# Up results of three groups written as whole rows, and two times moved in the column plan

## The chip, the cores and the metric

The kernel runs on one core of a Trainium2 chip. The metric is the device time of one execution in microseconds (us), before 4126.9 (median of 3 runs, 4126.24 to 4131.73). The engines of the core are TensorE (PE in the profile, its weight loads PEld), VectorE (DVE), ScalarE (ACT), GpSimd (POOL) and SyncE (SP), which here only issues transfers. Each takes its own instructions in the order in which the program emits them, and waits for others by semaphores.

## The reference

Two layers, each `x = x + conv(gn(x))` with x of shape (32, 48, 64, 128): batch, channels, height, width. `gn` normalizes each image over 16 groups of 3 channels. `conv` is four scans, each with a one-dimensional convolution of 5 taps over the 48 channels:

```python
def f(carry, inp):
    nxt = inp + _conv1d(carry, w, b)
    return (nxt, nxt)
```

It runs down the 64 rows (the convolution lies along the width), then up through the down results with the same weights, then right through the 128 columns (the convolution lies along the height), then left. A step needs the step ahead of it, so each scan is a chain.

## The kernel before

The batch of 32 is cut into four groups of 8 images (g = 0 to 3). A layer has six phases in `PHASES`: four of kind "rows", one for each group (63 down steps, then 63 up steps), and two of kind "cols", for groups 0 and 1 (pair 0) and groups 2 and 3 (pair 1), each with 127 right and 127 left steps. The names of the tiles of a step say layer, group or pair and way: `step_01d` is layer 0, group 1, down; `step_11r` is layer 1, pair 1, right. In layer 1 the groups 1 to 3 run an up scan and the next down scan in joint steps (`JOINED`). A step is 9 matmuls (L899), whose sums VectorE joins with the bias and the input by `scalar_tensor_tensor` (L913) into the row or column in the `arena`, a tile of SBUF with three slots; the next step reads that.

Between phases the data lies in DRAM. `xin` holds the permuted input of a group and `in_x` is the kernel's input before it is permuted; `upa` (layer 0) and `upb` (layer 1) hold the up results, one tensor per group; `mid` holds layer 0's result; `spill` takes a quarter of a pair that has no room; `held` holds results of layer 1 that are sent to `out` later. Numbers behind such names in a listing tell buffers apart: `upa2_90` is group 2 of layer 0, `spill1_103` is the spill of its pair 1.

In a row phase `move_rows` writes up results out, eight rows at a time. The three output blocks of 128 partitions are cut into ten pieces of 16 to 48 channels (`PIECES`), one transfer for each piece. A row of 128 floats (16 columns of 8 images, for one of the eight residues of the column) is cut into four quarters `q` of RUN = 32 floats, and `by_row` puts each at its own place in DRAM, in runs of 128 bytes, so that a quarter of the width lies together.

In a column phase the pair is worked in quarters j of 32 columns, each of six units of 128 x 2048 floats: `UNITS` is (block o, half), half 0 the first group of the pair, half 1 the second. `load_unit` reads one unit of quarter j by `by_col`; a partition's 2048 floats lie together there, 8 KB. The three slots hold three quarters; the first is written to `spill` (`spill_unit`) once its columns have been passed, and the fourth quarter is loaded in its place. In layer 0, on the way left, the residual is loaded for each unit (`load_residual`, from `xin`), added on GpSimd (`add_residual`, L834), and the unit is written to `mid` (`keep_result`); then `pair_scaling` works out the normalization of layer 1. In layer 1 the result is permuted and stored; residuals are loaded by ScalarE's queue there.

What sets the order is an agenda: `at(t, fn, ...)` asks for a piece of work ahead of step t, counted over all phases, and ahead of each step the pieces that are due are emitted, sorted by t and then by the order of asking. The numbers set only the order on each engine's queue. An instruction starts when those ahead of it on its engine have been issued and its semaphores allow it; nothing waits for a step as such. SyncE's queue carries nearly all transfers: row loads, up writes, input loads, unit loads, spills, residuals, results.

`plan_rows` sets row loads, scaling (`scale_rows`, L777, on ScalarE) and the up writes; for groups 0 to 2 of layer 0 four of the eight up writes come during the up scan, at steps 12, 20, 28 and 36 of it, and four in the next group's down scan, at 30, 42, 54 and 66 behind its start. `plan_input` prepares the input of the next groups in the same phases: `take_in` loads 2048 KB from `in_x`, GpSimd permutes it (L699), SyncE puts it out to `xin`, and ScalarE takes statistics of it (`take_others`, L562 and L570). `plan_cols` sets, with t0 the first right step, `left` the first left step and `end` the step behind the last: loads of the four quarters, spills at t0 + 33 + 2i for unit i, and the adds, in the order of the quarters 3, 2, 1, 0, the units of the first three at left + 34 + 32n + 4.5i. `after` holds for a pair that follows a pair: pair 1, in both layers.

Of the kernel before, what the change touches and what calls it, by code (L numbers as in the profile page):

```python
# [42 lines left out]
E8 = 8  # L43
FULL = 128
NG = E8 * C // FULL
NQ = 4
# [31 lines left out]
def weight_runs():  # L78
# [24 lines left out]
PHASES = (  # L103
    ("rows", 0, 0),
    ("rows", 0, 1),
    ("rows", 0, 2),
    ("rows", 0, 3),
    ("cols", 0, 0),
    ("cols", 0, 1),
    ("rows", 1, 0),  # L110
    ("rows", 1, 1),
# [3 lines left out]
    ("cols", 1, 1),  # L115
)
JOINED = (8, 9)


@with_exitstack  # L120
def kernel(
# [11 lines left out]
    NH = H // E8  # L133
# [3 lines left out]
    RUN = KQ * GB  # L137
# [89 lines left out]
    def by_row(t, e, h0, h1):  # L227


        t = t.rearrange("c (i q a e n) -> e a c i q n", i=E8, q=NQ, a=NH, e=E8)[e, h0 // E8]  # L230
        t = t[:, h0 % E8 : h0 % E8 + h1 - h0]
        return t.rearrange("c i q n -> c (i q) n")

    def x_by_row(t, e, h0, h1):

        t = t.rearrange("(i q) c (a e n) -> e a c i q n", i=E8, a=NH, e=E8)[e, h0 // E8]
        return t[:, h0 % E8 : h0 % E8 + h1 - h0].rearrange("c i q n -> c (i q) n")
# [44 lines left out]
    def by_col(t, e, j):  # L282


        return t.rearrange("c (i q n) -> i q c n", i=E8, q=NQ)[e, j]

    def dma(dst, src, queue=None):
        (queue or nc.sync).dma_start(dst, src)
# [21 lines left out]
    def pieces(o):  # L310
        return [(e, c0, c1, p0) for e, c0, c1, g, p0 in PIECES if g == o]
# [404 lines left out]
    def place(k, h):  # L716


        first = k
        while first in JOINED:  # L720
            first -= 1
# [5 lines left out]
    def rows_at(k, h0, h1):  # L727

        places = sorted(place(k, h) for h in range(h0, h1, E8))
        at = places[0] * E8 + h0 % E8  # L730
        assert h0 // HALF == (h1 - 1) // HALF and places[-1] - places[0] == len(places) - 1
        return row_views(k)[h0 // HALF][:, :, at : at + h1 - h0]
# [4 lines left out]
    def move_rows(k, h0, h1, to_dram):  # L737

        _, layer, g = PHASES[k]
        t = (ups if to_dram else source)[layer][g]  # L740
        for h in range(h0, h1, E8):
            end = min(h1, h + E8)
            view = rows_at(k, h, end)
            for o in range(NG):
                for e, c0, c1, p0 in pieces(o):
                    here = view[p0 : p0 + c1 - c0, o]
                    here = here.rearrange("p h (q n) -> p (h q) n", q=NQ)
                    if to_dram:
                        dma(by_row(t, e, h, end)[c0:c1], here)
                    else:  # L750
                        dma(here, (x_by_row if g else natural_row)(t, e, h, end)[c0:c1])
# [41 lines left out]
    def quarter(k, j):  # L793
        return slot[slots(k)[j % 3]].rearrange("p (o s n) -> p s o n", s=2, o=NG)

    def load_unit(k, j, i):


        _, layer, pair = PHASES[k]
        o, half = UNITS[i]  # L800
        unit = quarter(k, j)[:, half, o]
        t = ups[layer][2 * pair + half]
        for e, c0, c1, p0 in pieces(o):
            here = unit[p0 : p0 + c1 - c0]
            dma(here, by_col(t, e, j)[c0:c1])

    def spill_unit(k, i, back):
        _, layer, pair = PHASES[k]
# [190 lines left out]
    def scans(k):  # L999
        if PHASES[k][0] == "rows":  # L1000
            if k not in JOINED:
                for h in range(1, H):
                    yield 1, lambda h=h: row_step(k, h, row(k, h - 1), row(k, h), "d")
            end = last.rearrange("p (o n) -> p o n", o=NG)
            for h in range(H - 2, -1, -1):
                if k + 1 in JOINED:
                    yield 2, lambda h=h: two_row_step(k, h, k + 1, H - 1 - h)
# [13 lines left out]
    def at(t, fn, *args):  # L1021
        agenda.append((t, len(agenda), fn, args))

    def spread(t, gen, every):


        def go(t):
            if next(gen, "end") != "end":
                at(t + every, go, t + every)
                agenda.sort(key=lambda a: a[:2])  # L1030

        at(t, go, t)
# [21 lines left out]
    def plan_rows(k, t0, prev):  # L1054
        layer = PHASES[k][1]
        down, up = (2 if k in JOINED else 1), (2 if k + 1 in JOINED else 1)
        t_up = t0 + down * (H - 1)
# [4 lines left out]
        else:  # L1062
            ahead, scaled = (-54, -43, 0, 11), (-22, -8, 16, 30)
            if not PHASES[k][1]:
                ahead, scaled = (-36, -26, 0, 11), (-18, -8, 16, 30)
        if k in JOINED:
            for i in range(H // E8):
# [32 lines left out]
    def plan_cols(k, t0, prev):  # L1100
        _, layer, pair = PHASES[k]
        n = 2 * NG
        after = prev == "cols"
        for i in range(n):
            early = 30 if after else 58 if k - 1 in JOINED else 54
            at(t0 - early + 2 * i, load_unit, k, 0, i)
            at(t0 + (3 if after else -24 + 2 * i), load_unit, k, 1, i)
            at(t0 + (38 if after else 8) + 2 * i, load_unit, k, 2, i)
            at(t0 + 33 + 2 * i, spill_unit, k, i, False)
            at(t0 + 50 + 2 * i, load_unit, k, 3, i)  # L1110
        final = k == len(PHASES) - 1
        left = t0 + W - 1
        end = left + W - 1
        for i in range(n):

            t = left + 64 + 2 * i if layer == 0 else left + 39.5 + 4.5 * i
            at(t, spill_unit, k, i, True)
        units = []
        for n_done, j in enumerate((3, 2, 1, 0)):
            first, every = left + 34 + 32 * n_done, 4.5  # L1120
            if j == 0 and PHASES[k + 1 if not final else k][0] == "rows":
                first, every = (end + 29, 6) if pair else (first, 7)
            units += [(first + every * i, j, i) for i in range(n)]
        stats = None
        if layer == 0:
            stats = ResultStatsV(f"r{2 * pair}"), ResultStatsA(f"r{2 * pair + 1}")
        tiles = [stage[:, i] for i in range(4)]
        if layer:
            tiles += spare_tiles[0 : 2 if final else 1]
        n = len(tiles)  # L1130
        direct = [u for u in units if not (final and u[1] == 0)]

        for u, (t, j, i) in enumerate(direct):
            nat = tiles[u % n]
            o, half = UNITS[i]
            if u < n:
                at(left + 16, load_residual, k, j, i, nat)
            if layer == 0:
                if u >= n:
                    at(max(direct[u - n][0] + 3, t - 21), load_residual, k, j, i, nat)  # L1140
                at(t, add_residual, k, j, i, nat)
                at(t + 4, keep_result, k, j, i)
                unit = quarter(k, j)[:, half, o]
                if half == 0:
                    for b in range(GB):
                        at(t + 5 + b, stats[0].take, j, o, unit, b)
                else:
                    at(t + 1, stats[1].take, j, o, unit)
            else:

                at(t, add_residual, k, j, i, nat)
                at(t + 2.5, permute_unit, k, j, i, nat, (nc.gpsimd, nc.scalar, nc.scalar))
                if final or j not in HELD:
                    at(t + 4.5, store_result, k, j, i, nat)
                else:
                    at(t + 4.5, hold_result, j, i, nat)
                if final and j == 1:
                    at(t + 4.7, load_residual, k, 0, i, last_tiles(k)[i])

                if u >= 2 and u - 2 + n < len(direct):  # L1160
                    at(t + 4.6, load_residual, k, *direct[u - 2 + n][1:], tiles[(u - 2) % n])
        if layer == 0:
            spread(units[-1][0] + 14, pair_scaling(pair, stats, 8), 1)
        if layer:

            at(left + 10, nc.scalar.copy, junk[:, BN - 1 :], quarter(k, 3)[:, 0, 0, RUN - 1 : RUN])
        if layer and not final:
            todo = [(j, half, e) for j in HELD for half in range(2) for e in range(E8)]
            for n, what in enumerate(todo):
                at(end + 63 + 1.9 * n, let_result, *what)  # L1170
        if final:
            at(end + 4, last_results, k)

    def last_tiles(k):

        s = slot[slots(k)[2]].rearrange("p (i n) -> p i n", i=2 * NG)
        return [s[:, i] for i in range(2 * NG)]
# [10 lines left out]
    starts, end = [], 0  # L1188
    for k, (kind, *_) in enumerate(PHASES):
        n = (H if kind == "rows" else W) - 1  # L1190
        starts.append(end - 2 * n if k in JOINED else end)
        end = starts[-1] + (2 if k in JOINED else 1) * n + (2 if k + 1 in JOINED else 1) * n
    for k, (kind, layer, _) in enumerate(PHASES):
        (plan_rows if kind == "rows" else plan_cols)(k, starts[k], PHASES[k - 1][0])
# [279 lines left out]
```

## Time and profile before

| | |
|---|---|
| median of 3 runs | 4126.9 us (4126.24 to 4131.73) |
| the profiled execution's own time | 4129.71 us |
| its span, first to last instruction | 4128.0 us |
| mean granted TensorE clock | 0.990 of full speed |
| moved by DMA | 681.57 MB, mean 165 GB/s |
| packets under 512 B | 2008848 of 2207818 |

The trace is one execution. Rows of a timeline give start, duration, engine, line, operation, result <- operands, the shape, a count where rows are joined, and in brackets the idle time ahead with what ended it. SPq is SyncE's queue: a row there is the time in which transfers were issued, not moved. Rows of waits give who waited <- for whom: total, count, longest, in us.

```profile
PE   6999999999999999999999999999999999999994
...
PEclk9999999999999999999999999999999999999997
DMA  9898998986990399814896965666698029999799
```

Each digit is a fortieth of the span, 103 us: TensorE works in all of them, and the DMA engines are nearly full in the first third (the row phases of layer 0) and by stretches later.

### The profile page before, as it was taken

The numbers are of one execution on the slowest core, as the hardware profiler recorded it, in microseconds if no ns is written. First come the engines' busy times: TensorE is split into PE (matmuls) and PEld (weight loads), VectorE is DVE, ScalarE is ACT, GpSimd is POOL, SyncE is SP. The second block draws the span as 40 slices with busy tenths as digits, with TensorE's granted clock in tenths as the row PEclk, the third lists the DMA queues.
The fourth block names the chain that finished last, engine by engine and source line by source line (L and its number), as shares of the span: only waits on it lengthen the run. The fifth ranks groups of instructions, "written<-read, shape, count | busy, mean of one in ns | idle before, by whom it ended". The sixth has DMA issues, their size and how long they took to land. (4 is left out here: it accounts for less than half of the span.)

```text
span 4128.0 us, 85199 instructions
## 1 busy us (share of the span) xinstructions
PE 4015.7 (97%) x34360; PEld 3930.1 (95%) x34360; DVE 2082.2 (50%) x6137; ACT 1307.0 (32%) x2628; POOL 789.3 (19%) x672
## 2 busy tenths in 40 slices
PE   6999999999999999999999999999999999999994
PEld 5999999999999999999999998888999999999994
DVE  6454454544444567545656443333444444444444
ACT  4556547450000256003674633434000002300122
POOL 5631303200000243002411000000000015610353
PEclk9999999999999999999999999999999999999997
DMA  9898998986990399814896965666698029999799
GB/s 300 217 203 171 222 157 211 208 132 116 165 226 1 89 261 285 210 20 151 217 171 146 141 107 95 100 108 100 100 171 205 1 70 252 294 246 157 148 233 195
DMA packets 2207818, 681.57 MB, mean 165 GB/s; under 512 B 2008848, under 2 KB 2157504, under 8 KB 2182080
## 3 DMA queue, kind: packets, MB, share of 16 engines
q1 hardware_dynamic: 2071488, 595.36, 69.7%
q10 hardware_dynamic: 135936, 80.77, 8.1%
q8 instruction: 270, 4.42, 0.5%
q14 instruction: 124, 1.02, 0.1%
HBM read 399.11 MB, written 295.93 MB: 168 GB/s over the span
## 5 line engine op out<-in xcount | busy, mean ns | idle before, releaser
L834 POOL TENSOR_TENSOR arena<-arena 128x2048 f32<-128x2048 f32 x80 | 362.5, 4548 | 1714.7 <-PE step_00l L899 499.9
L777 ACT ACTIVATE arena<-arena,offsetr,scaler 128x128 f32<-128x128 f32 (+1 forms) x576 | 345.1, 687 | 348.4 <-DMA arena<-mid 291.0
L638 ACT ACTIVATE early<-arena 128x256 f32<-128x256 f32 x192 | 129.7, 676 | 816.0 <-POOL arena L834 809.6
L777 ACT ACTIVATE arena<-arena,offset,scale 128x256 f32<-128x256 f32 (+2 forms) x360 | 248.8, 785 | 151.4 <-DMA arena<-xin 143.2
L699 POOL COPY arena<-arena 128x256 f32<-128x256 f32 x340 | 201.0, 658 | 443.1 <-DMA arena<-in_x 392.5
L899 PE MATMUL step_01r<-arena,early 128*128 128x128 f32 x2286 | 249.8, 272 | 0.0
L899 PE MATMUL step_11r<-arena,early 128*128 128x128 f32 x2286 | 249.3, 272 | 0.0
L899 PEld LDWEIGHTS step_11r<-arena,early 128*128 128x128 f32 x2286 | 248.7, 184 | 0.6 <-DVE arena L913 0.3
L899 PEld LDWEIGHTS step_01r<-arena,early 128*128 128x128 f32 x2286 | 248.9, 184 | 0.2
L899 PE MATMUL step_00r<-arena,early 128*128 128x128 f32 x2286 | 248.5, 272 | 0.0
L899 PE MATMUL step_10l<-arena,wleft 128*128 128x128 f32 x2286 | 248.5, 272 | 0.0
L899 PE MATMUL step_11l<-arena,wleft 128*128 128x128 f32 x2286 | 248.5, 272 | 0.0
L899 PE MATMUL step_10r<-arena,early 128*128 128x128 f32 x2286 | 248.5, 272 | 0.0
L899 PEld LDWEIGHTS step_00r<-arena,early 128*128 128x128 f32 x2286 | 248.5, 184 | 0.0
L899 PE MATMUL step_00l<-arena,wleft 128*128 128x128 f32 x2286 | 248.4, 272 | 0.0
L899 PE MATMUL step_01l<-arena,wleft 128*128 128x128 f32 x2286 | 248.4, 272 | 0.0
L899 PEld LDWEIGHTS step_10l<-arena,wleft 128*128 128x128 f32 x2286 | 248.4, 184 | 0.0
L899 PEld LDWEIGHTS step_11l<-arena,wleft 128*128 128x128 f32 x2286 | 248.4, 184 | 0.0
L899 PEld LDWEIGHTS step_10r<-arena,early 128*128 128x128 f32 x2286 | 248.4, 184 | 0.0
L899 PEld LDWEIGHTS step_00l<-arena,wleft 128*128 128x128 f32 x2286 | 248.4, 184 | 0.0
L899 PEld LDWEIGHTS step_01l<-arena,wleft 128*128 128x128 f32 x2286 | 248.4, 184 | 0.0
L856 ACT COPY arena<-arena 128x256 f32<-128x256 f32 x172 | 99.7, 657 | 367.1 <-POOL arena L834 241.0
(545 smaller groups left out, 6880.6 us busy)
## 6 DMA issues: line engine op xcount, KB each, us to landing
xin<-arena SPq DMA_DIRECT2D x94, 512.0 KB, 5.1
arena<-in_x SPq DMA_DIRECT2D x18, 2048.0 KB, 10.0
upa<-arena SPq DMA_DIRECT2D x192, 192.0 KB, 4.1
arena<-upa SPq DMA_DIRECT2D x96, 384.0 KB, 11.7
arena<-xin SPq DMA_DIRECT2D x96, 384.0 KB, 10.7
upb<-arena SPq DMA_DIRECT2D x192, 192.0 KB, 3.9
arena<-upb SPq DMA_DIRECT2D x96, 384.0 KB, 11.1
arena<-xin SPq DMA_DIRECT2D x174, 192.0 KB, 4.3
```

The source lines that it names most:

```text
L638: nc.scalar.activation(junk[:, 0:n], view[:, b], AF.Identity, accum_out=self.sum[:, i, j : j + 1])
L699: copy(dst[:, r, q], src[:, r0 + r, q])
L777: nc.scalar.activation(args[0], args[0], AF.Identity, bias=args[2], scale=args[1])
L834: eng.tensor_tensor(unit, unit, nat, ALU.add)
L856: copy(by_w(perm)[:, a], src[:, a])
L899: nc.tensor.matmul(part(turn(whole(ps[o]))[0:m], -s), weights[:, i, at : at + m], part(turn(src(i)), s), start=seen[o] == 1, stop=seen[o] ...
```

## The change

There are three edits.

1. `WHOLE` names groups 0, 1 and 2 of layer 0. Their up results are written with `whole_row`: a row's four quarters stay together, in runs of 512 bytes. Their units are then read with `part_of_rows`: one quarter of each of 64 rows for each partition, 64 runs of 128 bytes in place of one of 8 KB. Group 3 and layer 1 keep the old layout.
2. In `plan_cols` the third quarter of a pair that follows a pair is loaded at t0 + 46 + 2i in place of t0 + 38 + 2i. The condition holds in layer 0 and in layer 1.
3. The last quarter (j = 0) of pair 0 in layer 0 is added at end + 10 + 6.5i in place of end + 3 + 4.5i. Residual loads, results and `pair_scaling` are set from the same numbers and move with it. Pair 1 keeps end + 29 + 6i; in layer 1 the numbers come out as before.

The arithmetic and its operations are the same.

```diff
+WHOLE = ((0, 0), (0, 1), (0, 2))
...
+    def whole_row(t, e, h0, h1):
+        t = t.rearrange("c (i a e n) -> e a c i n", i=E8, a=NH, e=E8)[e, h0 // E8]
+        return t[:, h0 % E8 : h0 % E8 + h1 - h0]
...
+    def part_of_rows(t, e, j):
+        return t.rearrange("c (i m q n) -> i q c m n", i=E8, q=NQ, n=RUN)[e, j]
...
+                    if to_dram and (layer, g) in WHOLE:
+                        dma(whole_row(t, e, h, end)[c0:c1], here)
+                        continue
...
-            dma(here, by_col(t, e, j)[c0:c1])
+            if (layer, 2 * pair + half) in WHOLE:
+                dma(here.rearrange("p (m n) -> p m n", n=RUN), part_of_rows(t, e, j)[c0:c1])
+            else:
+                dma(here, by_col(t, e, j)[c0:c1])
...
-            at(t0 + (38 if after else 8) + 2 * i, load_unit, k, 2, i)
+            at(t0 + (46 if after else 8) + 2 * i, load_unit, k, 2, i)
...
-            if j == 0 and PHASES[k + 1 if not final else k][0] == "rows":
-                first, every = (end + 29, 6) if pair else (first, 7)
+            if j == 0 and layer == 0:
+                first, every = (end + 29, 6) if pair else (end + 10, 6.5)
```

In the listings below, x2 and the like is a count of equal rows. SyncE's queue in the up scan of group 0, layer 0, holds the first up write of eight rows (before, L288):

```order
L288 DMA upa0_88<-arena_72 48x32x32 x2
L288 DMA upa0_88<-arena_72 32x32x32
L288 DMA upa0_88<-arena_72 16x32x32
L288 DMA upa0_88<-arena_72 48x32x32 x2
L288 DMA upa0_88<-arena_72 16x32x32
L288 DMA upa0_88<-arena_72 48x32x32 x2
L288 DMA upa0_88<-arena_72 32x32x32
```

At the same place stands after the change (the line has moved to L298):

```order
L298 DMA upa0_88<-arena_72 48x8x128 x2
L298 DMA upa0_88<-arena_72 32x8x128
L298 DMA upa0_88<-arena_72 16x8x128
L298 DMA upa0_88<-arena_72 48x8x128 x2
L298 DMA upa0_88<-arena_72 16x8x128
L298 DMA upa0_88<-arena_72 48x8x128 x2
L298 DMA upa0_88<-arena_72 32x8x128
```

The same ten transfers with the same bytes, in runs of 128 floats for 32; nothing has moved.

SyncE's queue in the right scan of pair 1, layer 0 (`step_01r`), from the first spill of the first quarter on, before:

```order
L288 DMA spill1_103<-arena_72 128x2048 x3
L288 DMA arena_72<-upa2_90 48x2048 x2
L288 DMA arena_72<-upa2_90 32x2048
L288 DMA spill1_103<-arena_72 128x2048
L288 DMA arena_72<-upa3_91 48x2048 x2
L288 DMA arena_72<-upa3_91 32x2048
L288 DMA spill1_103<-arena_72 128x2048
L288 DMA arena_72<-upa2_90 16x2048
L288 DMA arena_72<-upa2_90 48x2048 x2
L288 DMA arena_72<-upa2_90 16x2048
L288 DMA spill1_103<-arena_72 128x2048
L288 DMA arena_72<-upa3_91 16x2048
```

And after, from the last two spills on (four spills and two results of pair 0 stand ahead of them):

```order
L298 DMA spill1_103<-arena_72 128x2048 x2
L298 DMA arena_72<-upa2_90 48x64x32 x2
L298 DMA arena_72<-upa2_90 32x64x32
L298 DMA mid1_85<-arena_72 96x8x256
L298 DMA mid1_85<-arena_72 32x8x256
L298 DMA arena_72<-upa3_91 48x2048 x2
L298 DMA arena_72<-upa3_91 32x2048
L298 DMA arena_72<-upa2_90 48x64x32 x2
L298 DMA arena_72<-upa2_90 32x64x32
L298 DMA arena_72<-upa2_90 16x64x32
L298 DMA arena_72<-upa2_90 48x64x32 x2
L298 DMA arena_72<-upa2_90 16x64x32
```

All six spills now stand ahead of the third quarter's loads, one result of pair 0 (`mid1`) stands behind its first unit, and the second pair of rows of group 2 (48 x2, 32) is already the fourth quarter's first unit: from there the units of the two quarters alternate, the third quarter's last one behind four of the fourth, where before all six of the third came first.

SyncE's queue in the right scan of pair 1, layer 1 (`step_11r`), from the first spill on, before:

```order
L288 DMA spill3_105<-arena_72 128x2048 x3
L288 DMA arena_72<-upb2_94 48x2048 x2
L288 DMA arena_72<-upb2_94 32x2048
L288 DMA spill3_105<-arena_72 128x2048
L288 DMA arena_72<-upb3_95 48x2048 x2
L288 DMA arena_72<-upb3_95 32x2048
L288 DMA spill3_105<-arena_72 128x2048
L288 DMA arena_72<-upb2_94 16x2048
L288 DMA arena_72<-upb2_94 48x2048 x2
L288 DMA arena_72<-upb2_94 16x2048
```

And after:

```order
L298 DMA spill3_105<-arena_72 128x2048 x6
L298 DMA arena_72<-upb2_94 48x2048 x2
L298 DMA arena_72<-upb2_94 32x2048
L298 DMA arena_72<-upb3_95 48x2048 x2
L298 DMA arena_72<-upb3_95 32x2048
L298 DMA arena_72<-upb2_94 48x2048 x2
L298 DMA arena_72<-upb2_94 32x2048
L298 DMA arena_72<-upb2_94 16x2048
L298 DMA arena_72<-upb2_94 48x2048 x2
L298 DMA arena_72<-upb2_94 16x2048
```

Here too the six spills come first and the two quarters' units alternate (the second 48 x2, 32 of upb2 is the fourth quarter's); the layout of upb is as before.

## Prediction

> **What bounds the kernel now.** The page's engine totals come first, then the waits of TensorE, then the starts of the phases in VectorE's timeline.
>
> ```profile
> PE 4015.7 (97%) x34360; PEld 3930.1 (95%) x34360; DVE 2082.2 (50%) x6137; ACT 1307.0 (32%) x2628; POOL 789.3 (19%) x672
> ...
> PE step_01d L899 <- DVE arena L913: 6.8, 1, 6.8
> PE step_02d L899 <- DVE arena L913: 5.4, 1, 5.4
> ...
> 326.00 1.14 DVE L913 SCALAR_TENSOR_TENSOR arena<-step_01d,bd,arena 128x128 f32<-128x128 f32 x3 [0.91 <-DMA arena<-xin]
> 459.03 0.61 DVE L913 SCALAR_TENSOR_TENSOR arena<-step_01u,bd,arena 128x128 f32<-128x128 f32 x2 [0.73 <-PE step_01u L899]
> 588.10 0.61 DVE L913 SCALAR_TENSOR_TENSOR arena<-step_02d,bd,arena 128x128 f32<-128x128 f32 x2 [0.79 <-PE step_02d L899]
> 719.53 0.61 DVE L913 SCALAR_TENSOR_TENSOR arena<-step_02u,bd,arena 128x128 f32<-128x128 f32 x2 [0.73 <-PE step_02u L899]
> 847.08 0.61 DVE L913 SCALAR_TENSOR_TENSOR arena<-step_03d,bd,arena 128x128 f32<-128x128 f32 x2 [0.79 <-PE step_03d L899]
> 971.45 0.61 DVE L913 SCALAR_TENSOR_TENSOR arena<-step_03u,bd,arena 128x128 f32<-128x128 f32 x2 [0.73 <-PE step_03u L899]
> 1095.94 0.65 DVE L913 SCALAR_TENSOR_TENSOR arena<-step_00r,bd,arena 128x128 f32<-128x128 f32 x2 [0.78 <-DMA upa<-arena]
> 1344.26 0.61 DVE L913 SCALAR_TENSOR_TENSOR arena<-step_00l,bd,arena 128x128 f32<-128x128 f32 x2 [0.71 <-PE step_00l L899]
> 1592.60 1.18 DVE L913 SCALAR_TENSOR_TENSOR arena<-step_01r,bd,arena 128x128 f32<-128x128 f32 x3 [0.24 <-PE step_01r L899]
> 3574.41 1.11 DVE L913 SCALAR_TENSOR_TENSOR arena<-step_11r,bd,arena 128x128 f32<-128x128 f32 x3 [1.10 <-DMA arena<-mid]
> ```
>
> TensorE is busy for 97% of the span, so a gain can only be a phase that is longer than its steps. From start to start, 63 row steps take 124.37 us undisturbed (03d, 847.08 to 971.45: 1.975 a step), and 127 column steps 248.34 (00l: 1.956). Against that 01d (133.03) is 8.7 too long, 01u (129.07) 4.7, 02d (131.43) 7.1, 02u (127.55) 3.2. Beyond their one wait of 6.8 and 5.4, 01d and 02d lose 1.8 and 1.6 more; I read that as the slower steps behind a stop, and charge 1.8 for any new stop. Those 23.7 us are all that the change can win; everything else is cover to lose.
>
> What ends those waits stands in VectorE's, ScalarE's and SyncE's rows:
>
> ```profile
> 426.23 0.61 DVE L913 SCALAR_TENSOR_TENSOR arena<-step_01d,bd,arena 128x128 f32<-128x128 f32 x2 [7.10 <-DMA arena<-in_x]
> 408.37 17.83 ACT L777 ACTIVATE arena<-arena,offset,scale 128x256 f32<-128x256 f32 x24
> ...
> ACT early L570 <- DMA arena<-in_x: 9.8, 1, 9.8
> DVE neg_x_x L592 <- ACT early L562: 2.6, 1, 2.6
> ...
> 256.42 12.52 SPq L288 DMA_DIRECT2D upa<-arena  x10
> 289.89 11.10 SPq L288 DMA_DIRECT2D upa<-arena  x10
> 383.94 1.00 SPq L288 DMA_DIRECT2D arena<-in_x  x1
> ...
> 548.83 20.71 SPq L288 DMA_DIRECT2D upa<-arena  x20
> 615.07 1.31 SPq L288 DMA_DIRECT2D arena<-in_x  x1
> 655.33 0.61 DVE L913 SCALAR_TENSOR_TENSOR arena<-step_02d,bd,arena 128x128 f32<-128x128 f32 x2 [5.66 <-ACT arena L777]
> ```
>
> In 01d the step at 426.23 needs rows that ScalarE scales in the 17.83 us up to 426.2. ScalarE began late: it had waited 9.8 us for an input load (in_x), which SyncE issued at 383.94, behind group 0's up writes in its one queue. In 02d the same: the load of 615.07 stands behind 20 up writes of group 1. So transfers, not arithmetic, make both stops.
>
> **The change, part by part.** Prices of transfers, from windows in which the DMA engines were full (start:end, length, busy time of PE, PEld, DVE, ACT, POOL, granted clock, DMA share, GB/s):
>
> ```profile
> 270.00:289.00 19.00, 18.75 (x171) 18.56 (x170) 10.37 (x36) 3.70 (x5) 0.00 (x0) 1.00 1.00 152
> 1052.00:1070.00 18.00, 18.00 (x166) 18.00 (x165) 8.64 (x27) 0.00 (x0) 0.00 (x0) 1.00 0.99 152
> 1700.00:1712.00 12.00, 12.00 (x110) 11.85 (x109) 5.65 (x21) 0.00 (x0) 1.55 (x3) 1.00 1.01 216
> 1642.00:1650.00 8.00, 8.00 (x76) 8.00 (x75) 6.09 (x17) 6.56 (x18) 1.12 (x1) 1.00 1.04 346
> 1172.00:1180.00 8.00, 8.00 (x76) 8.00 (x75) 3.85 (x12) 0.00 (x0) 0.00 (x0) 1.00 1.01 423
> ```
>
> They are: row reads of xin in 128 B runs, up writes in 128 B runs, up reads in 8 KB runs, writes to mid in 1 KB runs, and spills. A unit (128 x 2048 floats, 1.049 MB) so costs 6.9 us read in 128 B runs, 4.9 in 8 KB runs, 3.0 in 1 KB runs, and 2.5 spilled.
>
> Part 1a, whole rows written. Eight rows of a group are 1.57 MB: 10.3 us at 152 GB/s. The trace has no 512 B run. Its bounds are 10.3 (no better than 128 B) and 4.5 (1 KB runs, 346); I take 5.2, near the lower, since a run of 512 B is nearer to 1 KB. Ten transfers are one such write, so two writes lie ahead of the load of 383.94 (256.42 and 289.89), and two ahead of that of 615.07. Two save 10.2, more than the 8.7 and 7.1 that are to be won: both stops go. With them goes VectorE's 2.6 behind ScalarE's statistics in 01u, and about 0.5 of 02u, which waits there too; the rest of these two phases, equal in both, has another cause and stays. Gain: 8.7 + 7.1 + 2.6 + 0.5 = **18.9**; ends 0 and 23.7.
>
> Part 1b, units read in 128 B runs. Groups 0 to 2 pay 6.9 instead of 4.9, bounds 4.9 and 9. In the first pair both halves pay, 2.0 x 6 = 12 for a quarter:
>
> ```profile
> 1103.47 3.02 SPq L288 DMA_DIRECT2D arena<-upa  x6
> 1134.27 23.71 SPq L288 DMA_DIRECT2D arena<-upa  x20
> ...
> arena<-upa SPq DMA_DIRECT2D x96, 384.0 KB, 11.7
> ```
>
> There the second quarter's last load is issued at 1106.5 and lands 11.7 later, at 1118; column 32 is due at 1095.94 + 31 x 1.956 = 1156.6, margin 38 against 24 for two quarters. The third lands at 1169.7, due at 1219: 49 against 36. The 128 B reads hide there, beside column steps that need no more than is there; if a read cost 9, they would just not.
>
> Parts 1b to 3 in the second pair (01r, S = 1592.60), where they meet:
>
> ```profile
> 1592.83 24.55 SPq L288 DMA_DIRECT2D arena<-upa  x20
> 1651.65 1.80 SPq L288 DMA_DIRECT2D spill<-arena  x3
> 1673.74 44.54 SPq L288 DMA_DIRECT2D arena<-upa  x30
> L834 POOL TENSOR_TENSOR arena<-arena 128x2048 f32<-128x2048 f32 x80 | 362.5, 4548 | 1714.7 <-PE step_00l L899 499.9
> ```
>
> Before, the third quarter is loaded between the spills, all of it ahead of the fourth. It is due with column 64, at S + 63 x 1.956 = S + 123. Six spills (15) and six units (29) from S + 59, and about 3 to land, give S + 106: 17 ahead. After: the second quarter takes 3 x 6.9 + 3 x 4.9 = 35, three residual loads and three results of pair 0 that now stand behind it (4.9 + 3.0 + 4.9, 3 x 3.0) 22, to S + 57, so the spills start with column 31, at S + 61, as they must. Six spills and the results kept among them (2 x 3.0) end at S + 82. Now the order counts: moved from 38 to 46 the third quarter's units alternate with the fourth's, and ahead of its last one's end stand five units of group 2 (34.5), five of group 3 (24.5) and one result (3.0): S + 144, landed S + 147. Due S + 123: **a stop of 24**, and 1.8 behind it. The adds themselves (4548 ns each on POOL, one per 6.5 steps or 12.7 us now) hide beside the steps; the sixth ends before S + 90, ahead of its result's place. Bounds of the stop: with reads at 4.9 the five units cost 34.5 - 24.5 = 10 less, and 14 stay; at 9 they cost 5 x 2.1 = 10.5 more, and the second quarter 6.3, of which the 4 us up to S + 61 hide the most: 37.
>
> Part 2 in layer 1. The edit is not bound to a layer, so 11r changes order too:
>
> ```profile
> 3634.00:3715.00 81.00, 81.00 (x745) 80.72 (x744) 39.81 (x124) 0.94 (x2) 0.00 (x0) 1.00 1.01 251
> 3633.54 1.78 SPq L288 DMA_DIRECT2D spill<-arena  x3
> 3658.64 45.82 SPq L288 DMA_DIRECT2D arena<-upb  x30
> arena<-upb SPq DMA_DIRECT2D x96, 384.0 KB, 11.1
> ```
>
> The DMA engines are full from the first spill on. The last load is issued by 3704.5 and lands 11.1 later, 3715.6. After, the third quarter's last unit has only two of the fourth behind it (9.8): it lands at 3705.8. Due: 3574.41 + 123.2 = 3697.6. **A stop of 8**, and 1.8. Worked forward from 3633.5 (15 + 10 x 4.9 + 3) it lands at 3700.5, a stop of 3; I take 8, since that count gives the whole stretch 15 + 12 x 4.9 = 74 us, and the window shows it full for 81. Bounds 0 and 12.
>
> Sum against the profiled run (4129.7, 1.7 of it outside the span): 4129.7 - 18.9 + 25.8 + 9.8 = 4146.4. The median of the runs shown is 2.8 lower; carried over, **4143.6**, say 4144. Its own range, with one term at a time at a bound: 4134 (the stop in 01r at 14, or none in 11r) to 4157 (the stop in 01r at 37).
>
> **Rivals.**
> A. The 128 B reads cost no more than the long ones (against it: 152 and 216 GB/s in full windows; for it: other rows, another tensor), and layer 1 stops for 3: -18.9 + 15.8 + 4.8 = +1.7, at 4129, no change. [...]
> B. Nothing stops: the third quarter lands ahead of its columns, because the queue runs ahead of my count. From the point at which the sum of both stops is under 8, it is faster: 4126.9 - 18.9 = 4108. For it: a 17 us margin before. Against it: 24 is far from 0, and both stretches already have a DMA share of 1.01.
> C. Reads in the new layout are dearer than those of xin, since a unit's 64 runs lie 512 bytes apart in a tensor that was just written. At 9.2 a unit, a third more, the stop in 01r is 24 + 5 x 2.3 + (3 x 2.3 - 4) = 38, and 1.8: 4126.9 - 18.9 + 40 + 9.8 = 4158. Against it: xin's rows are 128 B runs too, and took 6.9 a unit.
> D. The whole rows don't write faster, so that no stop goes: +35.6, at 4162. Against it: 346 GB/s at 1 KB beside 152 at 128 B. [...] No row of this trace has runs of 512 bytes.
>
> **Chances.** Forecast 0.62, A 0.19, B 0.11, C 0.05, D 0.03. A measurement can tell 0.2% (8.3 us, 4118.6 to 4135.2) from no change. The forecast's lower end (layer 1 without a stop: 4134) gives 0.08 of its chance to no change, B's upper end adds 0.02 to faster and takes it from A: faster 0.13, same 0.25, slower 0.62. The range 4114 to 4156 leaves out most of B, C and D, and a little of the forecast's upper end.
>
> **What would show it.** In 01d and 02d the waits of 6.8 and 5.4 gone, phases of 124 to 126 us. Windows of up writes of groups 0 to 2 near 300 GB/s. In 01r one wait of TensorE of about 24 us ahead of column 64, ended by DMA arena<-upa; in 11r one of about 8, ended by arena<-upb. Wrong would be: 01r near 251 us, or the writes still at 152.

## The result and the profile after

The changed kernel takes 4177.7 us (median of 4 runs, 4169.5 to 4180.5) against 4129.3 (median of 4, 4126.2 to 4132.3): a ratio of 1.0114, 95% interval 1.0096 to 1.0132. It is slower, as forecast, but by 48 us where 17 were forecast, and outside the range. The span of the profiled execution is 4178.7 us, 50.7 above that of before.

The page's engine totals, two rows of its slices, and the two longest waits of TensorE's steps in the changed kernel:

```profile
PE 4017.9 (96%) x34360; PEld 3931.9 (94%) x34360; DVE 2078.5 (50%) x6137; ACT 1306.7 (31%) x2628; POOL 789.1 (19%) x672
...
PE   6999999999999999599999999999999999989994
...
PEclk9999999999999999799999999999999999999997
...
PE step_01r L915 <- DVE arena L929: 51.0, 1, 51.0
PE step_11r L915 <- DMA arena<-upb: 15.6, 1, 15.6
```

The work of the engines is the same. Two new dents stand in the row of PE, the 5 at the seventeenth digit and the 8 at the fifth from the right, and they are the two waits. The waits in step_01d and step_02d are gone. The starts of the phases, in VectorE's timeline (L913 has become L929):

```profile
324.94 1.14 DVE L929 SCALAR_TENSOR_TENSOR arena<-step_01d,bd,arena 128x128 f32<-128x128 f32 x3 [0.91 <-PE step_01d L915]
449.26 0.61 DVE L929 SCALAR_TENSOR_TENSOR arena<-step_01u,bd,arena 128x128 f32<-128x128 f32 x2 [0.73 <-PE step_01u L915]
575.22 0.61 DVE L929 SCALAR_TENSOR_TENSOR arena<-step_02d,bd,arena 128x128 f32<-128x128 f32 x2 [0.79 <-DMA arena<-xin]
699.58 0.61 DVE L929 SCALAR_TENSOR_TENSOR arena<-step_02u,bd,arena 128x128 f32<-128x128 f32 x2 [0.73 <-PE step_02u L915]
825.54 0.61 DVE L929 SCALAR_TENSOR_TENSOR arena<-step_03d,bd,arena 128x128 f32<-128x128 f32 x2 [0.79 <-PE step_03d L915]
...
1571.30 0.78 DVE L929 SCALAR_TENSOR_TENSOR arena<-step_01r,bd,arena 128x128 f32<-128x128 f32 x2 [0.24 <-PE step_01r L915]
1746.38 0.61 DVE L929 SCALAR_TENSOR_TENSOR arena<-step_01r,bd,arena 128x128 f32<-128x128 f32 x2 [51.36 <-DMA arena<-upa]
1876.71 0.61 DVE L929 SCALAR_TENSOR_TENSOR arena<-step_01l,bd,arena 128x128 f32<-128x128 f32 x2 [0.71 <-PE step_01l L915]
3607.49 1.10 DVE L929 SCALAR_TENSOR_TENSOR arena<-step_11r,bd,arena 128x128 f32<-128x128 f32 x3 [1.10 <-DMA arena<-upb]
3874.43 0.61 DVE L929 SCALAR_TENSOR_TENSOR arena<-step_11l,bd,arena 128x128 f32<-128x128 f32 x2 [0.71 <-PE step_11l L915]
```

| phase | before | after | difference | forecast |
|---|---|---|---|---|
| 01d | 133.0 | 124.3 | -8.7 | -8.7 |
| 01u | 129.1 | 126.0 | -3.1 | -2.6 |
| 02d | 131.4 | 124.4 | -7.1 | -7.1 |
| 02u | 127.6 | 126.0 | -1.6 | -0.5 |
| 01r | 251.3 | 305.4 | +54.1 | +25.8 |
| 11r | 248.8 | 266.9 | +18.1 | +9.8 |

These six make +51.7; one microsecond is won ahead of 01d. So the gain came at about the forecast size (20.5 for 18.9), and both losses came where they were forecast, at twice the size. The stop in 01r ends at column 64 (1571.30 + 63 x 1.956 + 51.4 = 1745.9) with a load from upa, as forecast.

In SyncE's timeline the input load that had stood at 383.94 is issued 12.4 us earlier behind 01d's start than before (370.50 - 324.94 = 45.6, before 57.9). First the up writes ahead of it, two rows of before (L288) and four of after (L298), then the load, then windows at the last two of these writes (columns as in the prediction):

```profile
225.20 10.23 SPq L288 DMA_DIRECT2D upa<-arena  x10
239.83 12.74 SPq L288 DMA_DIRECT2D upa<-arena  x10
...
224.75 7.35 SPq L298 DMA_DIRECT2D upa<-arena  x10
235.89 9.80 SPq L298 DMA_DIRECT2D upa<-arena  x10
249.60 9.30 SPq L298 DMA_DIRECT2D upa<-arena  x10
280.08 6.80 SPq L298 DMA_DIRECT2D upa<-arena  x10
370.50 1.01 SPq L298 DMA_DIRECT2D arena<-in_x  x1
...
249.60:259.00 9.40, 9.40 (x89) 9.40 (x87) 5.87 (x23) 0.00 (x0) 0.00 (x0) 1.00 0.95 265
280.00:287.00 7.00, 7.00 (x66) 7.00 (x65) 3.24 (x10) 7.00 (x11) 0.00 (x0) 1.00 0.88 204
```

Four writes stand ahead of the load, not two. Before, they were issued in 46.6 us (the two above, and 12.52 and 11.10), after in 33.3: 13.3 saved, 3.3 a write. Counted from the span's start the load comes 13.4 earlier (383.94 and 370.50), so these writes make all of it. The windows show 265 and 204 GB/s (other transfers run at the edges of both), where near 300 was expected.

In 01r, SyncE's rows, and then the windows in which only up reads run (the first two in step_00r, the others in 01r and 11r):

```profile
1581.30 41.23 SPq L298 DMA_DIRECT2D arena<-upa  x20
...
1640.17 2.87 SPq L298 DMA_DIRECT2D spill<-arena  x1
...
1656.61 7.52 SPq L298 DMA_DIRECT2D spill<-arena  x2
...
1681.13 70.22 SPq L298 DMA_DIRECT2D arena<-upa  x37
...
1141.00:1186.00 45.00, 45.00 (x416) 45.00 (x416) 22.11 (x69) 0.00 (x0) 0.00 (x0) 1.00 1.17 139
1204.00:1249.00 45.00, 45.00 (x416) 45.00 (x416) 22.15 (x71) 0.00 (x0) 0.00 (x0) 1.00 1.14 136
1700.00:1740.00 40.00, 0.00 (x0) 0.00 (x0) 0.00 (x0) 0.00 (x0) 0.00 (x0) 0.50 1.31 155
3690.00:3720.00 30.00, 30.00 (x279) 30.00 (x278) 14.89 (x47) 0.00 (x0) 0.00 (x0) 1.00 1.03 184
```

The second quarter's loads start at 1581.30, 10.0 us behind the phase's start, where before they started at 0.2; they are being issued for 41.2 us (24.6 before), and the spills begin 68.9 us behind the phase's start in place of 59.1. Reads in 128 B runs from upa go at 139 and 136 GB/s in the first two windows, not at the 152 of xin's rows. The third window, 155, holds both kinds. In 11r the 8 KB reads go at 184.

### The profile page after: what moved, and what is told of

It reads as the page before. It is cut to its first block, busy times and chain, and to the rows that moved or that the text cites. A ratio compares the mean times of both kernels' runs of the same rounds, so it can differ in the third digit from the quotient of the medians.

```text
span 4178.7 us, 85181 instructions
## 1 busy us (share of the span) xinstructions
PE 4017.9 (96%) x34360; PEld 3931.9 (94%) x34360; DVE 2078.5 (50%) x6137; ACT 1306.7 (31%) x2628; POOL 789.1 (19%) x672
## 5 line engine op out<-in xcount | busy, mean ns | idle before, releaser
L915 PEld LDWEIGHTS step_01r<-arena,early 128*128 128x128 f32 x2286 | 251.7, 185 | 51.4 <-DVE arena L929 51.2
L915 PE MATMUL step_11r<-arena,early 128*128 128x128 f32 x2286 | 251.9, 274 | 15.6 <-DMA arena<-upb 15.6
L915 PE MATMUL step_00r<-arena,early 128*128 128x128 f32 x2286 | 248.8, 272 | 0.0
```

The lines of the kernel that those rows point to most:

```text
L915: nc.tensor.matmul(part(turn(whole(ps[o]))[0:m], -s), weights[:, i, at : at + m], part(turn(src(i)), s), start=seen[o] == 1, stop=seen[o] ...
```

## The experiments

Each kernel ran beside the kernel before on the same chip; times are medians, with the ratio to before. All are edits of the changed kernel but where it says otherwise. Stops are waits of TensorE in the profile.

| run | time | ratio (95%) | stop in 01r | stop in 11r |
|---|---|---|---|---|
| the change | 4177.7 | 1.0114 (1.0096 to 1.0132) | 51.0 | 15.6 |
| e1 | 4159.8 | 1.0080 (1.0066 to 1.0094) | 51.2 | none |
| e2 | 4151.8 | 1.0062 (1.0048 to 1.0075) | 38.8 | none |
| e3 | 4136.9 | 1.0026 (1.0014 to 1.0038) | 15.1 | 11.2 |
| e4 | 4128.8 | 1.0003 (0.9994 to 1.0012) | 17.2 | none |
| e5 | 4107.2 | 0.9953 (0.9940 to 0.9967) | none | none |
| e6 | 4156.7 | 1.0072 (1.0057 to 1.0087) | 10.0 | 15.0 |
| e7 | 4172.0 | 1.0112 (1.0097 to 1.0127) | 48.4 | 12.3 |
| e8 | 4129.8 | 1.0008 (0.9999 to 1.0018) | 20.1 | none |
| e9 | 4131.5 | 1.0012 (1.0002 to 1.0021) | 17.6 | none |
| e10 | 4148.2 | 1.0049 (1.0034 to 1.0064) | 36.3 | none |
| e11 | 4171.4 | 1.0102 (1.0085 to 1.0119) | 44.8 | 15.7 |

Two theories stood at the start: the order of the loads makes the stops, or the 128 B reads do.

**e1: the third quarter at 38 in layer 1.**

```diff
-            at(t0 + (46 if after else 8) + 2 * i, load_unit, k, 2, i)
+            at(t0 + ((38 if layer else 46) if after else 8) + 2 * i, load_unit, k, 2, i)
```

> The third quarter goes back to t0 + 38 in layer 1 alone; layer 0 keeps all of the change. If layer 1's stop (15.6 us in step_11r) comes from the order on SyncE's queue alone, step_11r has no wait over 1 us and the time falls by 15.6 and some 3 of slow steps, to 4159. Rival: the stop comes from what layer 0's new layout or the later phases leave behind (another place in DRAM, a later start); then it stays, and the time is 4178.

e1 is 33.8 us above the kernel before that ran beside it (4126.0), the change 48.4 above its own (4129.3): 14.6 less, and no stop in 11r. Layer 1's loss is the order of its loads alone.

**e2: the third quarter at 38 in both layers, the later sums kept.**

```diff
-            at(t0 + (46 if after else 8) + 2 * i, load_unit, k, 2, i)
+            at(t0 + (38 if after else 8) + 2 * i, load_unit, k, 2, i)
```

> The third quarter goes back to t0 + 38 in both layers; the whole rows and the later, wider sums stay. If the order makes both stops, step_11r has none and step_01r's 51 us shrink to what the dearer reads and the results among the loads leave: the last unit of the third quarter then has 5 units less ahead of it, some 5 x 6.7 = 33 us, so a stop of about 15 to 20, and a time of 4125 to 4130. Rival: the 128 B reads make the stop in step_01r by themselves; then it stays above 40, and the time is 4155 or more.

Neither: 4151.8 and 38.8 us. VectorE's row at the end of the stop shows why:

```profile
1704.26 0.62 DVE L625 BATCH_NORM_STATS2 bn_r<-arena 128x6 f32<-128x256 f32 x1 [39.44 <-DMA arena<-upa]
```

It is not a step that waits here but a statistic of pair 0's last quarter. Its unit 4 is summed at end + 36, its statistics of images 6 and 7 are asked for at end + 47 and 48, and the third quarter's unit 4 is loaded into the same place at end + 46. In this kernel these two statistics are therefore taken of the loaded data, so it computes something else there, and VectorE waits for the load with the steps queued behind. So e2 says nothing of the order's price. It shows that the later sums need the later load.

**e4 and e5: whole rows alone**, of three groups and of two; the times as in the kernel before.

```diff
-            at(t0 + (46 if after else 8) + 2 * i, load_unit, k, 2, i)
+            at(t0 + (38 if after else 8) + 2 * i, load_unit, k, 2, i)
...
-            if j == 0 and layer == 0:
-                first, every = (end + 29, 6) if pair else (end + 10, 6.5)
+            if j == 0 and PHASES[k + 1 if not final else k][0] == "rows":
+                first, every = (end + 29, 6) if pair else (first, 7)
```

and for e5 also

```diff
-WHOLE = ((0, 0), (0, 1), (0, 2))
+WHOLE = ((0, 0), (0, 1))
```

> Whole rows of three groups alone; the third quarter at 38 and the sums as before. If the layout is a gain that the other two edits lose again: stops of 01d and 02d gone (20 us), step_01r with a stop of 0 to 10 us (before, the third quarter was about 15 us early; the second and third quarters have three dearer units each, 6 x 2 = 12 us), time 4108 to 4120. Rival: the 128 B reads of the second pair cost the 51 us: time above 4150.

> Whole rows of groups 0 and 1 alone, so that the second pair reads 8 KB runs as before; the third quarter and the sums as before. The writes that lie ahead of the late input loads are those of groups 0 and 1, so both stops of the row phases should go (20 us) with nothing against it: 4107 to 4110, step_01r as before at 251 us. Rival: the first pair's twelve dearer units for a quarter are not hidden, or group 2's writes were needed for the gain: a stop in step_00r or 03d, and 4115 or more.

e5 did what was hoped, 4107.2: no stop in 01d or 02d, none in 01r. Group 2's whole rows, the only difference to e4, gain nothing (03d and 03u were undisturbed before, 124.4 and 124.5 us) and cost 21.6 us. e4's stop of 17.2 is not the late third quarter either; VectorE's row and GpSimd's add ahead of it:

```profile
1641.47 0.62 DVE L625 BATCH_NORM_STATS2 bn_r<-arena 128x6 f32<-128x256 f32 x1 [17.86 <-POOL arena L850]
...
1636.94 4.49 POOL L850 TENSOR_TENSOR arena<-arena 128x2048 f32<-128x2048 f32 x1 [40.02 <-DMA arena<-xin]
```

The statistic waits for an add, and the add for a residual that stands in SyncE's queue behind the second quarter's loads. With group 2's 128 B reads these loads take longer (issued for 38.4 us, 24.6 in the kernel before), the residual comes late, and VectorE stops with the steps behind the statistic, at column 27. The later, wider sums keep that stop away. In the changed kernel an add on GpSimd waits as long for its residual, and no step does:

```profile
1635.66 4.54 POOL L850 TENSOR_TENSOR arena<-arena 128x2048 f32<-128x2048 f32 x1 [41.88 <-DMA arena<-xin]
```

**e3: two groups, the moved times kept**, and **e6: the moved times alone** (WHOLE empty).

```diff
-WHOLE = ((0, 0), (0, 1), (0, 2))
+WHOLE = ((0, 0), (0, 1))
...
-WHOLE = ((0, 0), (0, 1), (0, 2))
+WHOLE = ()
```

> The change with the old layout for group 2: the second pair reads 8 KB runs only, and the two moved times stay. If the stop of 51 us in step_01r is mostly order, it shrinks only by what the 128 B reads cost in it: by the prices of full windows 5 x 2.0 of the alternating units and a little of the second quarter, so 35 to 40 stay, and the time is about 4165. If it is the layout, 10 or less stay and the time is about 4135.

> The two moved times alone, every group in the old layout. If the order makes the stops, step_11r stops for 15.6 as in the change, step_01r for 35 to 40, and the row phases lose their 23 us as before: 4185 to 4195. If the stop in step_01r needs the 128 B reads, it is 10 or less there and the time is about 4155.

With 8 KB reads in the second pair the stops in 01r are 15.1 and 10.0. e3 differs from the change in group 2's layout alone, so this layout makes about 36 of the change's 51 us, and the two moved times together the rest; no run parts these two in 01r, and the 5 us between e3 and e6 are not explained. The expectation, order 35 to 40, had it the wrong way round. SyncE's rows in e3 that answer to those of the change (S = 1572.96):

```profile
1571.25 27.27 SPq L298 DMA_DIRECT2D arena<-upa  x20
...
1632.02 0.34 SPq L298 DMA_DIRECT2D spill<-arena  x1
...
1639.48 6.25 SPq L298 DMA_DIRECT2D spill<-arena  x2
```

The second quarter starts 1.7 us ahead of the phase (the change: 10.0 behind), is issued for 27.3 us (41.2), and the spills start at 59.1 with column 31 (68.9). By the trace the last spill lands at S + 84.7, in the change at S + 104.8: 20 of the 36 us are there before the first unit of the third quarter is read. The other 16 are the five units of group 2 that alternate with the fourth quarter, 3.2 each.

**e7: the same units ahead, not alternating.**

```diff
-            at(t0 + 50 + 2 * i, load_unit, k, 3, i)
+            at(t0 + (45 + 0.2 * i if after and i < 4 else 50 + 2 * i), load_unit, k, 3, i)
```

> The change, but four units of the fourth quarter come as one block ahead of the third quarter, in place of alternating with it: the last unit of the third quarter has the same units ahead of it. If reads that alternate between two quarters are slow (176 GB/s in step_11r, 213 in the kernel before, where the quarters follow one another), reads rise to about 210 and the stop in step_11r falls from 15.6 to about 6; time 4165. If the slow reads have nothing to do with the mixing, the stop stays at 15 and the time at 4178.

11r stops for 12.3, 01r for 48.4 (in two stops, both for units of the third quarter). The alternating isn't what makes the reads slow: e3 alternates in layer 1, with the same instructions there as the change, and stops for 11.2. Between executions of one and the same layer 1 (the change, e3, e6, e11) the stop is 11.2 to 15.7, so 12.3 can't be told from 15.6.

**e8: the fourth quarter later.**

```diff
-            at(t0 + 50 + 2 * i, load_unit, k, 3, i)
+            at(t0 + (60 if after else 50) + 2 * i, load_unit, k, 3, i)
```

> The change, with the fourth quarter at t0 + 60 in place of 50, so that the third quarter is whole ahead of it and still behind all spills. If the place among the fourth quarter's units makes the stops, step_11r has none (landing at about 111 us behind the phase's start, due at 123), and step_01r's shrinks by 5 units, about 33 us, to 15 or 20: time 4122 to 4130. If being behind the spills makes them, both stay: 4178.

As expected: none in 11r, 20.1 in 01r (31 less), 4129.8. It is the units of the fourth quarter ahead, not the place behind the spills, that makes layer 1's stop. What is left in 01r is the price of group 2's layout: by the trace the last spill lands at S + 103.8, about as late as in the change, and the third quarter, three units of group 2 among its six, follows by S + 143.8, where column 64 is due at S + 123.

**e9 and e10, on e4: the units by group, and all four groups whole.** The question left open was whether 128 B reads are dear or make the 8 KB reads among them dear.

```diff
+            u = (0, 2, 4, 1, 3, 5)[i] if after and not layer else i
-            at(t0 + (3 if after else -24 + 2 * i), load_unit, k, 1, i)
+            at(t0 + (3 if after else -24 + 2 * i), load_unit, k, 1, u)
...
-WHOLE = ((0, 0), (0, 1), (0, 2))
+WHOLE = ((0, 0), (0, 1), (0, 2), (0, 3))
```

(the first two lines, and the same for the other quarters, are e9; the last is e10)

> As e4 (whole rows of three groups alone, a stop of 17.2 us in step_01r), but in the second pair of layer 0 the three units of group 2 (128 B runs) are loaded ahead of the three of group 3 (8 KB runs), in place of one by one. If 8 KB reads are slow only while 128 B reads run among them, the second quarter takes 3 x 8.0 + 3 x 4.9 = 39 us in place of the 45 to 48 seen, the third as much less, and the stop falls to about 3; time 4113. Rival: the price is in the bytes of group 2 alone (some 10 to 11 us a unit), and the order within a quarter is nothing; then the stop stays at 15 to 20, time 4129.

> As e4, with group 3 too written as whole rows, so that the second pair reads 128 B runs only. If 8 KB reads among 128 B reads already go at their pace (131 GB/s for the mixture, as for the first pair's pure 128 B reads), six more dearer units cost next to nothing, and the stop in step_01r stays at 15 to 20; time about 4129. Rival: prices add up, 8.0 against 4.9 for each unit; then three units in each of the second and third quarter and the first one's backlog bring 6 x 3.1 = 19 us or more, a stop of 36 or more, time 4148.

e9's stop didn't move (17.6), and e10's rose to 36.3, the rival's figure: prices add up, and each layout has its own. The 17.6 and 34.5 of the 36.3 are the statistic at column 27, as in e4, not the third quarter that e9's expectation had in mind; the other 1.8 of e10 come later, at the third quarter. But the price shows in the second quarter too, which by the trace takes from first issue to last landing 44.0 us by group (e9), 44.9 in turn (e4), and 52.7 with six units in 128 B runs (e10). The added three units cost 2.6 each. In e9 the two kinds stand apart, the 8 KB reads of group 3 first behind the 128 B reads:

```profile
1615.00:1626.00 11.00, 8.32 (x77) 8.13 (x75) 4.55 (x13) 0.00 (x0) 0.00 (x0) 1.00 1.02 209
```

209 GB/s, close to the 216 of before. Mixing is not the cause.

**e11: the change without the later sums.**

```diff
-            if j == 0 and layer == 0:
-                first, every = (end + 29, 6) if pair else (end + 10, 6.5)
+            if j == 0 and PHASES[k + 1 if not final else k][0] == "rows":
+                first, every = (end + 29, 6) if pair else (first, 7)
```

> The change without its third edit: whole rows of three groups, the third quarter at t0 + 46, the sums as before. With e4 (17.2), e2 (38.8) and the change (51.0) it fills the square of the two moved times in step_01r. If the moved times cost the same whatever the other does (the later sums 21.6, the later third quarter 12.2), the stop is 29, and step_11r stops for 11 to 16 as in the change: 4150 to 4160. If they share the same free time, so that either alone costs nearly as much as both, the stop is 40 to 50, and the time 4165 to 4175.

44.8 in 01r, in two stops, VectorE's rows at their ends:

```profile
1642.44 0.62 DVE L625 BATCH_NORM_STATS2 bn_r<-arena 128x6 f32<-128x256 f32 x1 [21.18 <-POOL arena L850]
...
1743.27 0.61 DVE L929 SCALAR_TENSOR_TENSOR arena<-step_01r,bd,arena 128x128 f32<-128x128 f32 x2 [24.54 <-DMA arena<-upa]
```

First the statistic, then the third quarter. The later sums take the first away, and the time saved is waited for at column 64: together 51.0. (The sum of parts that the expectation worked with rests on e2, which is no measure.)

## Why the prediction was right in kind and wrong in size

**Right.** The gain: both stops in the row phases were transfers in SyncE's queue, and went with whole rows, 20.5 us for the 18.9 forecast. That its size fits is in part luck: the forecast saved 5.1 us on each of two writes ahead of 01d's load, the runs show 3.3 on each of four. Two at 3.3 make 6.7, no more than the stop of 6.8 itself. The places of both losses, what ends them and at which column. That the first pair hides its 128 B reads: no stop in 00r. Rival D (whole rows write no faster) fell with that, rival B (nothing stops) with the first profile. That part 2 acts in layer 1 as well: e1.

**Wrong, in 01r: "After: the second quarter takes 3 x 6.9 + 3 x 4.9 = 35 [...] to S + 57, so the spills start with column 31, at S + 61, as they must."** Two things in this step failed.

- The price of 6.9 us for a unit in 128 B runs came from xin's rows. Up reads in the new layout cost 7.6 (139 and 136 GB/s in step_00r), and 3.2 more than an 8 KB unit in 01r. So reads in the new layout are dearer than those of xin, as rival C (0.05) had it. Its price of 9.2 was too high, and no run tests its reason, the 512 bytes from run to run.
- The step begins at S, as in the kernel before. But the first quarter of the second pair, loaded ahead of S in the same queue, holds three units of group 2 too. The text left them out, so the second quarter started 10 us late (in e3, with the old layout of group 2, 1.7 us ahead of S), and the slack ahead of the spills was used up.

Counted anew, eleven units of group 2 stand ahead of the end of the third quarter's last one: three each of the first, second and third quarter, two of the fourth. At 3.2 that is 35, and e3 against the change measures 36. The forecast had 5 x 2.0 = 10 for the same; the rest of its stop, 14 "with reads at 4.9", is what e3 and e6 show (15.1 and 10.0). So the part of the moved times was right, and the layout's part too small by 26.

**Wrong, in 11r: "Worked forward from 3633.5 (15 + 10 x 4.9 + 3) it lands at 3700.5 [...]; I take 8".** Only the size: 15.6, in other executions of the same instructions 11.2 and 15.0. By the trace the last spill lands at S + 79.9, not at 74, and the ten units behind it take 59 us, 5.9 each, where 4.9 came from one window of 12 us (1700 to 1712, 216 GB/s). The window of 30 us above shows 184. Why these reads are slower than the 200 to 216 of other stretches isn't settled; e7 speaks against the alternating.

**Wrong, a little: 1.8 us for the slow steps behind a stop.** 54.1 - 51.0 = 3.1 in 01r and 2.5 in 11r. Windows of 2 us show the granted clock third from the right: first behind the stop in 01d before, which ended at 426.23, then behind the stop in 01r:

```profile
428.00:430.00 2.00, 2.00 (x12) 2.00 (x11) 0.70 (x2) 1.94 (x6) 2.00 (x5) 0.50 0.16 56
430.00:432.00 2.00, 2.00 (x20) 2.00 (x20) 0.96 (x3) 1.91 (x6) 2.00 (x4) 1.00 0.62 209
...
1746.00:1748.00 2.00, 1.21 (x6) 1.21 (x7) 0.61 (x2) 0.00 (x0) 0.00 (x0) 0.50 1.63 107
1748.00:1750.00 2.00, 2.00 (x11) 2.00 (x11) 0.70 (x2) 0.00 (x0) 0.00 (x0) 0.50 1.27 155
1750.00:1752.00 2.00, 2.00 (x12) 2.00 (x11) 0.35 (x1) 0.00 (x0) 0.00 (x0) 0.50 1.25 206
1752.00:1754.00 2.00, 2.00 (x17) 2.00 (x17) 1.04 (x3) 0.00 (x0) 0.00 (x0) 0.83 0.99 205
1754.00:1756.00 2.00, 2.00 (x21) 2.00 (x20) 0.96 (x3) 0.00 (x0) 0.00 (x0) 1.00 0.99 224
```

In 01r half clock for some 6 us from the end of the stop, so about 3 lost. In 01d it lasted about 4 us (426.2 to 430.0; 0.50 in the window from 426 to 428 too), and 1.8 were lost; the forecast carried that over to the new stops. In 11r the windows from 3747 to 3753 show 0.50, 0.50 and 0.53, the next 1.00: some 6 us again. So half clock lasted 4 us behind the wait of 6.8 and 6 us behind those of 51.0 and 15.6; what sets its length these runs don't show.

**Not foreseen at all:** the third edit has a purpose that the prediction gave it no price for. It keeps VectorE's statistics from waiting for late residuals (17.2 us in e4 without it). The prediction worked out the adds on GpSimd and found them hidden, and didn't ask what is queued behind a statistic on VectorE. In the changed kernel this hides nothing in the end, since column 64 waits for longer.

## What to carry to other kernels

A layout that makes writes cheap and reads dear (here 3.3 us less for a write of eight rows and 3.2 more for a unit in 01r) is worth trying for each tensor by itself: it paid for groups 0 and 1, whose writes are waited for, and not for group 2 (e5, 4107.2, faster than both kernels). When a transfer gets dearer, count every one of its kind in the queue ahead of the deadline, those ahead of the phase's start too, since a backlog is handed on: in 01r the second quarter's loads started 10.0 us late, and the spills began at 68.9 in place of 59.1. And a load that is moved later by a number in a plan is also moved past its neighbours: read from the queue's order what then stands ahead of it, in every phase in which the number is used.

## What the runs showed of the hardware

Reads of 128 B runs did not have one price: 152 GB/s for xin's rows (270 to 289 in the kernel before), 136 to 139 for quarters of whole rows 512 bytes apart. It made little difference where in its row a quarter begins: the third quarter (256 bytes into the row) went at 139, the fourth (384) at 136. In these two windows the DMA share is 1.17 and 1.14, where xin's rows showed 1.00; what makes the difference is open.
